# Edge scores of a graph layer's second stage moved from SBUF to a PSUM bank, and output stores that reuse a loaded register

## The chip, the cores and the metric

The kernel runs on one core of one Trainium2 chip. The metric is the device time of one execution in microseconds (us). Engines carry the profile's names: PE (matmuls), PEld (weight loads), DVE (VectorE), ACT (ScalarE), POOL (GpSimd) and SP (SyncE, which here only issues DMAs).

## What is computed

Two graph layers follow each other, each with a residual sum and a layer norm. There are 12500 nodes with 64 features and 200000 edges, sorted by destination. The change lies in the second layer, whose reference is, cut to what matters:

```python
Z = jnp.einsum('ni,rio->nro', h, fc_weight)        # 8 relations
z_s, z_d = Z[src, etype], Z[dst, etype]
aw = attn_weight[etype, :, 0]
e = relu(sum(concatenate([z_s, z_d], axis=1) * aw, axis=1))   # the score of an edge
m = segment_max(e, dst)
ex = exp(e - m[dst])
alpha = ex / segment_sum(ex, dst)[dst]
h_out = segment_sum(alpha[:, None] * z_s, dst)
x = layernorm(x + h_out)
```

So each edge has a score `e`, the maximum of the scores over the edges of one destination is subtracted, and the exponentials weigh the source rows.

## The kernel before

Edges are cut into chunks of 128 (one edge a partition). Four chunks are a run, two runs are a group, so a group is 8 chunks or 1024 edges, and there are 196 groups (`NG`). The destinations of a run lie in a window of `W` = 96 neighbouring nodes, so a sum or a maximum over destinations becomes work with 0/1 matrices of 128 edges by 96 nodes.

The first layer's loop (`sum0` and `finish0`, lines 480 to 506) writes a row of 65 numbers for each node and relation into `z_tab` in DRAM. The second layer's loop (lines 687 to 724) then runs over the 196 groups with `sum1`, and over 106 output tiles of 125 nodes with `finish1` and `scale1`. All are generators: each `yield` ends a piece, and the calls of `group(...)` and `node(...)` in lines 695 to 718 are the order of all instructions, written out by hand (`tc.manual_schedule()`), so that pieces of up to six groups stand between each other. Each engine works through its own instructions in that order.

What a group does, in `sum1`:

- POOL gathers the source rows: eight indirect DMAs a group, one for each chunk (line 311), into `zg`, which has 5 buffers; the index lists `row_i` lie in SBUF. Group i+3 is gathered while group i is worked on. SP loads the window's rows `dw` (line 530) and the row of relative destinations (line 444).
- PE and ACT build the transposed 0/1 matrix `ohT` (lines 539 to 543), DVE builds the 0/1 matrix `oh`, 128 x 768 (`choose`, line 305), out of a ramp of numbers `iota_n` that lies in the PSUM tile `psc`[...].
- DVE makes the scores `e`, 128 x 8 in SBUF: L560 sums the destination's part, L562 adds the source's part out of `zg` and is the first instruction of a group that waits for the gathers, and L563 takes the maximum with 0.
- DVE multiplies `oh` with the scores in two products of 128 x 384 (line 571): the first into the SBUF tile `oe`, the second into columns 128 to 511 of `psc`. L573 to L575 take the maximum over the four chunks of a run.
- The maximum over edges follows through a PE transpose (L580) and L585, and through L595 and L596 it meets the maxima `top` that were kept so far. L596 (`d`, 65 x 96, two for each group) subtracts one SBUF tile from another.
- L616 reads each edge's maximum out of PSUM into `em`, L617 subtracts it from `e`, ACT takes the exponential (L620) and scales `zg` with it (L622), PE sums over edges (L626), and L630 and L631 update the sums `acc` (SBUF) with numbers out of PSUM.

`finish1` loads a tile's rows `xn` at a node number that SP loads into a register out of `slot_row` (`slot`, line 431), and later computes the unscaled output `y`. For four tiles at once `scale1` takes the root and stores them: for each store SP loads the same node number out of `slot_row` again (line 670).

Of the kernel before, what the change touches and what calls it, by code (L numbers as in the profile page):

```python
# [29 lines left out]
AF = mybir.ActivationFunctionType  # L30
OP = mybir.AluOpType
AX = mybir.AxisListType
ENG = mybir.EngineType
PSUM = bass.MemoryType.PSUM

N, E, D, DE, NR = 12500, 200000, 64, 32, 8
P = 125
EC = 128
NT = N // P
KS = 4  # L40
RE = KS * EC
S = 2
K = S * KS
# [6 lines left out]
W = 96  # L50
# [10 lines left out]
def gnn_kernel(ctx: ExitStack, tc, x, xT, src, dstp, dst, et, eaT, u, W1, b1, W2, b2, fc, aw, out):  # L61
    nc = tc.nc
# [21 lines left out]
    iota = consts.tile([128, 128], F32, name="iota")  # L84
# [19 lines left out]
    nc.vector.memset(ones_row, 1.0)  # L104
    psc = fixed.tile([128, 512], F32, name="psc")

    nc.vector.tensor_copy(psc[:, :128], iota)
    iota_n, iota_r = psc[:EC, :W], psc[:EC, :NR]

    w1x = consts.tile([D, 2, D], F32, name="w1x")  # L110
# [45 lines left out]
    for j in range(4):  # L156
        s = slice(j * (N // 4), (j + 1) * (N // 4))
# [10 lines left out]
    with (  # L168
# [54 lines left out]
        at = pre.tile([NQ, RQ], F32, name="at")  # L223
# [54 lines left out]
    def window_of(row, at, *engines):  # L278
        return nc.values_load(row[0:1, at], engines=engines, min_val=0, max_val=N - 1,
                              skip_runtime_bounds_check_because="a destination, so a node")  # L280
# [149 lines left out]
    def slot(i):  # L430
        return lambda engine: nc.values_load(
            slot_row[0:1, i - FIRST:i - FIRST + 1], engines=[engine], min_val=0, max_val=N - P,
            skip_runtime_bounds_check_because="the first node of a tile")

    def span(g):

        n = min(S, NRE - g * S)
        return n, min(n * KS, NCE - g * K), slice(g * K, g * K + n * KS)

    def row_load(work, g):  # L440
        def load():
            n = span(g)[0]
            row = work.tile([1, n, RE], BF16, name="row", bufs=4)
            nc.sync.dma_start(row, rel_tab[g * S:g * S + n, :].rearrange("(o s) e -> o s e", o=1))
            return row
        return load

    def wins_load(g):
        return lambda engine: [window_of(base_row, slice(g * S + s, g * S + s + 1), engine) for s in range(span(g)[0])]

    def all_of(pieces):
        for _ in pieces:
            pass
# [10 lines left out]
    groups, slots = {}, {}  # L464
# [9 lines left out]
    with (  # L474
# [4 lines left out]
        psum = Banks(pool, {"po": "small", "pw": "small"})  # L479
        for i in range(-3, NG + 2):  # L480
            g = i + 3
            if g < NG:
                n, chunks, c = span(g)
# [39 lines left out]
    for t in (acc, top):  # L523
        nc.scalar.copy(t, none[:D + 1].to_broadcast([C, N + W]))

    def sum1(work, psum, n, chunks, idx, rel_of, et_of, row_of, wins_of):
        row = row_of()
        dw = work.tile([W, n, Q], BF16, name="dw", bufs=4)
        for s, b in enumerate(wins_of(ENG.SP)):
# [15 lines left out]
        pq = psum.tile([EC, n * KS, Q], F32, name="pq")  # L545
        for k in range(n * KS):
            s, i = divmod(k, KS)
            nc.tensor.matmul(pq[:, k, :], ohT[:, s, i * EC:(i + 1) * EC], dw[:, s, :], start=True, stop=True)
        yield
        oh = choose(work, rel_of, n, bufs=3)  # L550
# [8 lines left out]
        e = work.tile([EC, n * KS], F32, name="e")  # L559
        nc.vector.tensor_reduce(e, ed.rearrange("p k j r -> p k (j r)"), AX.X, OP.add)  # L560
        yield
        nc.vector.tensor_add(e, e, zg[:, :, D])  # L562
        nc.vector.scalar_tensor_tensor(e, e, 0.0, pq[:, :, 3 * NR], OP.max, OP.mult)  # L563


        half = KS // 2
        by_run, es = oh.rearrange("p (s i) w -> p s i w", s=n), e.rearrange("p (s i) -> p s i", s=n)
        oe = work.tile([EC, n, half, W], F32, name="oe")
        other = psc[:EC, 128:128 + n * half * W].rearrange("p (s i w) -> p s i w", s=n, i=half)
        for to, i in ((oe, slice(0, half)), (other, slice(half, KS))):  # L570
# [39 lines left out]
        for k in range(n * KS):  # L610
            s, i = divmod(k, KS)
# [2 lines left out]

        em = work.tile([EC, n * KS], F32, name="em")
        nc.vector.tensor_reduce(em, pm, AX.X, OP.add)  # L616
        nc.vector.tensor_sub(e, e, em)  # L617
        nc.scalar.activation(factor, d, AF.Exp)  # L618
        wz = work.tile([EC, n * KS, C], F32, name="wz")
        nc.scalar.activation(wz[:, :, D], e, AF.Exp)  # L620
        for k in range(n * KS):
            nc.scalar.activation(wz[:, k, :D], zg[:, k, :D], AF.Copy, scale=wz[:, k, D:])  # L622
        yield
        for k in range(n * KS):
            s, i = divmod(k, KS)
# [5 lines left out]
            nc.vector.tensor_add(mine, mine, sums[:, s, :])  # L631


    def finish1(work, psum, n0_of, y_of):

        n0 = n0_of(ENG.SP)
        xn = work.tile([P, D], F32, name="xn1", bufs=5)
        nc.sync.dma_start(xn, x1_tab[ds(n0, P), :])
        yield
        n0 = n0_of(ENG.Activation)  # L640
        own = work.tile([C, P], F32, name="own")
        nc.scalar.copy(own, acc[:, ds(n0, P)])
        yield
        pl = psum.tile([P, C], F32, name="pl")
        nc.tensor.transpose(pl, own, ident[:C, :C])
        yield
        y, mv = y_of()
        den = work.tile([P, 1], F32, name="den")

        nc.vector.tensor_scalar_max(den, pl[:, D:], 1e-30)  # L650
        nc.vector.reciprocal(den, den)
        nc.vector.scalar_tensor_tensor(y, pl[:, :D], den, xn, OP.mult, OP.add)
        st = work.tile([P, nc.vector.BN_STATS_DIM], F32, name="ln_st")
        nc.vector.bn_stats(out=st, in_=y)
        nc.vector.bn_aggr(out=mv, in_=st)

    def scale1(work, n0s_of, y, mv):
        n = len(n0s_of)
        v = work.tile([P, n], F32, name="ln_v")
        nc.scalar.activation(v, mv[:, :n, 1], AF.Sqrt, bias=eps)  # L660
        back = work.tile([1, 1], F32, name="back")
        nc.scalar.activation(back, none[:1], AF.Exp)  # L662
        yield
        nc.vector.reciprocal(v, v)
        shift = work.tile([P, n], F32, name="ln_shift")
        nc.vector.scalar_tensor_tensor(shift, mv[:, :n, 0], -1.0, v, OP.mult, OP.mult)
        yield
        for j, n0_of in enumerate(n0s_of):
            nc.scalar.activation(y[:, j, :], y[:, j, :], AF.Identity, bias=shift[:, j:j + 1], scale=v[:, j:j + 1])  # L669
            nc.sync.dma_start(out[ds(n0_of(ENG.SP), P), :], y[:, j, :])  # L670

    with (
        tc.tile_pool(name="l1", bufs=2) as work,
        tc.tile_pool(name="l1_ps", bufs=1, space=PSUM) as pool,
        tc.manual_schedule(),
    ):
        psum = Banks(pool, pq=2, pb=2)
        groups, slots, ys, scales = {}, {}, {}, {}

        def y_of(i):  # L680
            q, at = divmod(i - FIRST, NQ1)
            if at == 0:
                ys[q] = (work.tile([P, NQ1, D], F32, name="y1"),
                         work.tile([P, NQ1, nc.vector.BN_AGGR_DIM], F32, name="ln_mv"))
            return ys[q][0][:, at, :], ys[q][1][:, at, :]

        for i in range(-3, NG + 4):
            g = i + 3
            if g < NG:
                n, chunks, c = span(g)  # L690
                groups[g] = sum1(work, psum, n, chunks, row_i[:, c], rel[:, c], et_i[:, c],
                                 row_load(work, g), wins_load(g))
            if FIRST <= i < NG:
                slots[i] = finish1(work, psum, slot(i), lambda i=i: y_of(i))
            group(i + 3)
            node(i)
            group(i)
            group(i - 1)
            group(i + 2)
            group(i + 1)  # L700
            group(i + 2)
            node(i - 3)
            group(i)
            group(i + 2)
            group(i - 1)
            group(i - 1)
            group(i + 1)
            group(i)
            group(i)
            group(i - 1)  # L710
            group(i - 2)
            group(i - 1)
            group(i)
            node(i - 3)
            for q in scales:
                next(scales[q], None)
            group(i)
            node(i - 2)
            for q in scales:
                next(scales[q], None)  # L720
            q, at = divmod(i - 3 - FIRST, NQ1)
            if FIRST <= i - 3 < NG and (at == NQ1 - 1 or i - 3 == NG - 1):
                scales = {q: scale1(work, [slot(j) for j in range(i - 3 - at, i - 2)], *ys[q])}
                next(scales[q])

    with (
        tc.tile_pool(name="r1", bufs=1) as work,
        tc.tile_pool(name="r1_ps", bufs=1, space=PSUM) as psum,
    ):
        def more1(r, w):  # L730
            idx, rl, row, base = further(work, r, w)
            chunks = ds(r * KS, KS)
            etx = work.tile([EC, KS], I32, name="x_et")
            nc.vector.tensor_copy(etx, et_i[:, chunks])
            nc.vector.tensor_copy(idx, row_i[:, chunks])
            all_of(sum1(work, psum, 1, KS, idx, rl, etx, lambda: row, lambda engine: [base]))

        def node1(at):
            y = work.tile([P, 1, D], F32, name="y1")
            mv = work.tile([P, 1, nc.vector.BN_AGGR_DIM], F32, name="ln_mv")  # L740
            all_of(finish1(work, psum, lambda engine: at, lambda: (y[:, 0, :], mv[:, 0, :])))
            all_of(scale1(work, [lambda engine: at], y, mv))

        leftover(more1, node1)

# [41 lines left out]
```

## Time and profile before

| | |
|---|---|
| median of 3 runs | 4121.7 us (4120.01 to 4121.73) |
| the profiled execution | 4110.41 us, its span 4108.6 us |
| second layer's gathers on POOL | first starts at 2088.1 us, last at 4070.6 us; 1563, busy 1507.6 us |
| 2300 to 3100 us: busy of 800 us | PE 510, DVE 573, ACT 426, POOL 608 us |
| 3100 to 4000 us: busy of 900 us | PE 608, DVE 720, ACT 590, POOL 684 us |
| L571, first and second product | 558 and 560 ns, 195 full groups |
| L596 | 255 ns, 391 times |

In a group line of the profile the two numbers behind the first bar are the summed busy time in us and the mean of one instruction in ns; behind the second bar stands the idle time of the engine just before these instructions and what ended most of it. "issue" means that the engine waited for nothing that the profile shows. In a timeline the first number is the start in us from the span's start, the second the duration in us, and the bracket tells the idle time before. The profiled execution is 11.3 us shorter than the median of the timed runs.

### The profile page before, as it was taken

To read this page: it belongs to the slowest core of one execution; us is meant where nothing else is said; L and a number is where in the kernel's file an instruction comes from. 1 tells how busy PE (TensorE), PEld (TensorE's weight loads), DVE (VectorE), ACT (ScalarE), POOL (GpSimd) and SP (SyncE) were. 2 spreads that over 40 slices of the span, in tenths; PEclk is the share of its full clock that TensorE was granted. 3 is DMA by queue.
4 is the path that set the end of the run, shared out by engine and by line. 5 is a ranking of instruction groups with operands and counts; after the bars stand their busy time and mean duration, and the time that the engine had idled before them with its cause. 6 is when DMAs were issued, how large, how long until landed. Compare 5 with 4: busy or idle time off the path is not lost. (4 is left out here: it accounts for less than half of the span.)

```text
span 4108.6 us, 63192 instructions
## 1 busy us (share of the span) xinstructions
PE 2993.0 (73%) x16301; PEld 2321.8 (57%) x16302; DVE 2440.2 (59%) x8117; ACT 1432.1 (35%) x3693; POOL 2995.2 (73%) x3141
## 2 busy tenths in 40 slices
PE   4666776667899999999946666666567766666675
PEld 4555565556676777777735444444455544554454
DVE  3333333333555555555547777777778778878786
ACT  0000000000111111111155555555556666666665
POOL 1677777777777777777757777777777777777774
PEclk9655555555656555565555556555655556555655
DMA  5211111111333333333311111111111111111111
GB/s 132 53 45 45 46 45 45 45 46 46 73 78 78 77 78 78 81 80 78 75 37 29 29 29 28 28 29 28 29 31 35 35 35 35 35 34 36 34 36 26
DMA packets 316692, 201.40 MB, mean 49 GB/s; under 512 B 239185, under 2 KB 239315, under 8 KB 315966
## 3 DMA queue, kind: packets, MB, share of 16 engines
q0 software_dynamic: 100032, 103.43, 13.0%
q1 hardware_dynamic: 201039, 87.74, 8.6%
q10 hardware_dynamic: 15249, 6.10, 0.6%
q8 instruction: 132, 2.16, 0.2%
q14 instruction: 240, 1.97, 0.2%
HBM read 155.15 MB, written 41.84 MB: 48 GB/s over the span
## 5 line engine op out<-in xcount | busy, mean ns | idle before, releaser
L311 POOL DMA_INDIRECT bg<-b_tab,src_i x1563 | 1475.2, 944 | 574.6 <-issue 435.2
L311 POOL DMA_INDIRECT zg<-z_tab,row_i x1563 | 1507.6, 965 | 501.4 <-issue 423.1
L363 PE MATMUL pa<-oh,msg 128*64 128x96 f32 x3128 | 536.7, 364 | 276.0 <-ACT msg L358 273.2
L358 ACT ACTIVATE msg<-msg 128x512 f32<-128x512 f32 x196 | 123.2, 628 | 1709.1 <-DVE msg L357 1676.2
L353 PEld LDWEIGHTS pm<-aw,cb 128*128 128x128 f32 x3128 | 604.9, 297 | 138.6 <-issue 137.8
L363 PEld LDWEIGHTS pa<-oh,msg 128*64 128x64 f32 x3128 | 480.1, 222 | 297.6 <-ACT msg L358 291.1
L353 PE MATMUL pm<-aw,cb 128*128 128x64 f32 x3128 | 639.0, 389 | 0.0
L626 PE MATMUL pb<-oh,wz 128*65 128x96 f32 x3128 | 549.7, 369 | 16.1 <-ACT wz L622 3.0
L357 DVE TENSOR_TENSOR msg<-pm,bg 128x512 f32<-128x512 f32 x196 | 135.3, 690 | 698.9 <-DMA bg<-b_tab,src_i 553.7
L626 PEld LDWEIGHTS pb<-oh,wz 128*65 128x65 f32 x3128 | 494.6, 229 | 72.8 <-ACT wz L622 72.8
L622 ACT ACTIVATE wz<-zg,wz 128x64 f32<-128x64 f32 x1564 | 394.7, 335 | 6.7
L305 DVE TENSOR_TENSOR oh<-psc,rel 128x768 f32<-128x768 f32 x392 | 370.6, 945 | 12.3 <-DMA row<-rel_tab 9.5
L580 PE MATMUL pt<-ident,t 128*96 128x128 f32 x391 | 123.5, 419 | 326.6 <-DVE mq L375 326.3
L540 ACT ACTIVATE off<-ps_row,minus_p 96x512 bf16<-96x512 f32 x391 | 265.8, 680 | 264.1 <-PE ps_row L539 264.0
L539 PE MATMUL ps_row<-row,ones_row 1*96 1x512 bf16 x391 | 210.4, 538 | 196.5 <-ACT off L540 186.0
L369 DVE TENSOR_TENSOR xa<-xa,pa 64x96 f32 x391 | 100.8, 258 | 327.0 <-PE pa L363 319.5
L587 PE MATMUL pt<-ident,m 96*65 96x96 f32 x782 | 176.6, 380 | 159.6 <-DVE m L585 159.6
L580 PEld LDWEIGHTS pt<-ident,t 128*96 128x96 f32 x391 | 50.8, 184 | 418.6 <-issue 395.1
L348 DVE TENSOR_SCALAR cb<-ps_row,iota_p 96x1024 f32<-96x1024 f32 x196 | 246.1, 1256 | 9.0 <-PE ps_row L299 9.0
L587 PEld LDWEIGHTS pt<-ident,m 96*65 96x65 f32 x782 | 119.6, 220 | 176.8 <-DVE m L585 176.8
L299 PE MATMUL ps_row<-row,ones_row 1*96 1x512 bf16 x391 | 197.8, 604 | 17.5 <-DMA row<-rel_tab 16.2
L543 ACT ACTIVATE ohT<-off 96x1024 bf16<-96x1024 bf16 x196 | 206.6, 1054 | 6.3
(140 smaller groups left out, 3613.5 us busy)
## 6 DMA issues: line engine op xcount, KB each, us to landing
z_tab<-z SPq DMA_DIRECT2D x106, 253.9 KB
bg<-b_tab,src_i POOLq DMA_INDIRECT x1563
zg<-z_tab,row_i POOLq DMA_INDIRECT x1563
cb<-in_eaT SPq DMA_DIRECT2D x195, 128.0 KB
aw<-a_tab SPq DMA_DIRECT2D x391, 24.0 KB
dw<-d_tab SPq DMA_DIRECT2D x391, 4.7 KB
row<-rel_tab SPq DMA_DIRECT2D x390, 2.0 KB
xn<-in_x SPq DMA_DIRECT2D x106, 31.2 KB
```

The costliest lines, as they stand in the source:

```text
L299: nc.tensor.matmul(ps[:, s, :RE], ones_row, row[:, s, :], start=True, stop=True)
L305: nc.vector.tensor_tensor(oh, iota_n[:, None, :].to_broadcast([EC, n * KS, W]), rel_of.unsqueeze(2).to_broadcast([EC, n * KS, W]), OP.is_e ...
L311: nc.gpsimd.indirect_dma_start(out=to[:, k, :], out_offset=None, in_=table[:, :], in_offset=bass.IndirectOffsetOnAxis(ap=idx[:, k:k + 1], ...
L348: nc.vector.tensor_scalar(cb[:W, :, :], ps_row, iota_p[:W], None, OP.is_equal)
L353: nc.tensor.matmul(pm[:, k, :], cb[:, s, i * EC:(i + 1) * EC], aw_t[:, s, :], start=True, stop=True)
L363: nc.tensor.matmul(pa[D:, s, :], msg[:, k, :], oh[:, k, :], start=(i == 0), stop=(i == KS - 1))
L539: nc.tensor.matmul(ps_row[:, :RE], ones_row, row[:, s, :], start=True, stop=True)
L540: nc.scalar.activation(off[:, s, :], ps_row[:, :RE], AF.Abs, bias=minus_p[:W])
L543: nc.scalar.activation(ohT, off, AF.Relu, bias=1.0, scale=-1.0)
L587: nc.tensor.matmul(rows[:, s, :], m[:, s:s + 1].to_broadcast([W, C]), ident[:W, :W], start=True, stop=True)
L622: nc.scalar.activation(wz[:, k, :D], zg[:, k, :D], AF.Copy, scale=wz[:, k, D:])
L626: nc.tensor.matmul(sums[:, s, :], wz[:, k, :], oh[:, k, :], start=(i == 0), stop=(i == KS - 1))
```

## The change

The scores of a group leave L563 into columns 96 to 103 (even group) or 104 to 111 (odd group) of the PSUM tile `psc`, no longer into the SBUF tile `e`. Both products and the later subtraction (L617) read them there. The subtraction's result goes into `em`, and ACT's exponential reads `em`. The ramp copied into `psc` is cut from 128 to 96 columns to make room. Apart from that, `finish1` hands on the register with the node number, and `scale1` stores with it, so that the second register load for each store is gone.

```diff
-    nc.vector.tensor_copy(psc[:, :128], iota)
+    nc.vector.tensor_copy(psc[:, :W], iota[:, :W])
...
-    def sum1(work, psum, n, chunks, idx, rel_of, et_of, row_of, wins_of):
+    def sum1(work, psum, n, chunks, idx, rel_of, et_of, row_of, wins_of, odd=0):
...
         nc.vector.tensor_add(e, e, zg[:, :, D])
-        nc.vector.scalar_tensor_tensor(e, e, 0.0, pq[:, :, 3 * NR], OP.max, OP.mult)
+        score = psc[:EC, W + odd * K:W + odd * K + n * KS]
+        nc.vector.scalar_tensor_tensor(score, e, 0.0, pq[:, :, 3 * NR], OP.max, OP.mult)
...
-        by_run, es = oh.rearrange("p (s i) w -> p s i w", s=n), e.rearrange("p (s i) -> p s i", s=n)
+        by_run, es = oh.rearrange("p (s i) w -> p s i w", s=n), score.rearrange("p (s i) -> p s i", s=n)
         oe = work.tile([EC, n, half, W], F32, name="oe")
         other = psc[:EC, 128:128 + n * half * W].rearrange("p (s i w) -> p s i w", s=n, i=half)
         for to, i in ((oe, slice(0, half)), (other, slice(half, KS))):
             nc.vector.tensor_mul(to, by_run[:, :, i, :], es[:, :, i].unsqueeze(3).to_broadcast([EC, n, half, W]))
...
-        nc.vector.tensor_sub(e, e, em)
+        nc.vector.tensor_sub(em, score, em)
...
-        nc.scalar.activation(wz[:, :, D], e, AF.Exp)
+        nc.scalar.activation(wz[:, :, D], em, AF.Exp)
...
-    def finish1(work, psum, n0_of, y_of):
+    def finish1(work, psum, n0_of, y_of, tell=lambda n0: None):
...
         nc.sync.dma_start(xn, x1_tab[ds(n0, P), :])
+        tell(n0)
...
-        for j, n0_of in enumerate(n0s_of):
+        for j, n0 in enumerate(n0s):
...
-            nc.sync.dma_start(out[ds(n0_of(ENG.SP), P), :], y[:, j, :])
+            nc.sync.dma_start(out[ds(n0, P), :], y[:, j, :])
...
-                slots[i] = finish1(work, psum, slot(i), lambda i=i: y_of(i))
+                slots[i] = finish1(work, psum, slot(i), lambda i=i: y_of(i), lambda n0, i=i: places.update({i: n0}))
...
-                scales = {q: scale1(work, [slot(j) for j in range(i - 3 - at, i - 2)], *ys[q])}
+                scales = {q: scale1(work, [places[j] for j in range(i - 3 - at, i - 2)], *ys[q])}
```

More of the change, by code (lines that the diff above doesn't have):

```diff
@@ L655, in finish1, with scale1 @@
         nc.vector.bn_aggr(out=mv, in_=st)
-    def scale1(work, n0s_of, y, mv):
-        n = len(n0s_of)
+    def scale1(work, n0s, y, mv):
+        n = len(n0s)
         v = work.tile([P, n], F32, name="ln_v")
@@ L677, in gnn_kernel @@
         psum = Banks(pool, pq=2, pb=2)
-        groups, slots, ys, scales = {}, {}, {}, {}
+        groups, slots, ys, scales, places = {}, {}, {}, {}, {}
         def y_of(i):
@@ L691, in gnn_kernel @@
                 groups[g] = sum1(work, psum, n, chunks, row_i[:, c], rel[:, c], et_i[:, c],
-                                 row_load(work, g), wins_load(g))
+                                 row_load(work, g), wins_load(g), g % 2)
             if FIRST <= i < NG:
-                slots[i] = finish1(work, psum, slot(i), lambda i=i: y_of(i))
+                slots[i] = finish1(work, psum, slot(i), lambda i=i: y_of(i), lambda n0, i=i: places.update({i: n0}))
             group(i + 3)
@@ L741, in node1 @@
             all_of(finish1(work, psum, lambda engine: at, lambda: (y[:, 0, :], mv[:, 0, :])))
-            all_of(scale1(work, [lambda engine: at], y, mv))
+            all_of(scale1(work, [at], y, mv))
         leftover(more1, node1)
```

## The prediction

> **What bounds the kernel now.** I read the page first: its groups, then the list of waits, then the timeline of single engines in the second layer, since the change touches nothing that runs often before it (the ramp's copy runs once, at 285 ns). On the page the dearest group after 2088 us is the gathers:
>
> ```profile
> span 4108.6 us, 63192 instructions
> ...
> L311 POOL DMA_INDIRECT zg<-z_tab,row_i x1563 | 1507.6, 965 | 501.4 <-issue 423.1
> ```
>
> 1507.6 us busy and 501.4 us idle fill the stretch from 2088.1 us to 4071.8 us, in which the last gather ends (25.3 us of the idle time is the stage's begin). So POOL does nothing else there, and its idle time is said to wait for nothing. The list of waits confirms who waits for whom:
>
> ```profile
> POOL zg L311 <- issue: 423.1, 1306, 25.3
> ...
> DVE e L562 <- DMA zg<-z_tab,row_i: 245.0, 182, 2.2
> ```
>
> In 182 of 196 groups DVE stands at L562 until the gathers have landed, 1.39 us in the median. The next view is POOL's timeline of one group and a bit:
>
> ```profile
> 3000.34 0.94 POOL L311 DMA_INDIRECT zg<-z_tab,row_i  x1 [0.30 <-issue]
> 3001.59 0.94 POOL L311 DMA_INDIRECT zg<-z_tab,row_i  x1 [0.30 <-issue]
> 3002.83 0.94 POOL L311 DMA_INDIRECT zg<-z_tab,row_i  x1 [0.30 <-issue]
> 3004.08 1.11 POOL L311 DMA_INDIRECT zg<-z_tab,row_i  x1 [0.30 <-DMA zg<-z_tab,row_i]
> 3005.50 0.94 POOL L311 DMA_INDIRECT zg<-z_tab,row_i  x1 [0.31 <-issue]
> 3006.74 0.94 POOL L311 DMA_INDIRECT zg<-z_tab,row_i  x1 [0.30 <-issue]
> 3007.99 0.94 POOL L311 DMA_INDIRECT zg<-z_tab,row_i  x1 [0.30 <-issue]
> 3009.24 0.94 POOL L311 DMA_INDIRECT zg<-z_tab,row_i  x1 [0.30 <-issue]
> 3010.49 0.95 POOL L311 DMA_INDIRECT zg<-z_tab,row_i  x1 [0.30 <-issue]
> ```
>
> The reader is to see two things. The gap is 0.30 us whatever the bracket says: over all 1563 gathers it never exceeds 0.32 us after the first, so no buffer and no DMA holds POOL (a `zg` buffer has been free for 10.7 us or more when its gather starts). And one gather in eight, the third of a group, takes 1.11 us instead of 0.94. Its mean over 196 groups is 1103 ns; the other positions have a median of 944 ns. The excess over 944 ns of all 1563 gathers is 1507.6 - 1563 x 0.944 = 32.1 us, of which 196 x 0.159 = 31.2 us is the third one's. What ran on DVE in that stretch:
>
> ```profile
> 3002.95 0.17 DVE L562 TENSOR_TENSOR e<-e,zg 128x8 f32<-128x8 f32 x1 [1.40 <-DMA zg<-z_tab,row_i]
> 3003.15 0.16 DVE L563 SCALAR_TENSOR_TENSOR e<-e,pq 128x8 f32<-128x8 f32 x1
> 3003.35 0.56 DVE L571 TENSOR_TENSOR oe<-oh,e 128x384 f32<-128x384 f32 x1
> 3003.83 0.56 DVE L571 TENSOR_TENSOR psc<-oh,e 128x384 f32<-128x384 f32 x1
> ...
> 3006.13 0.95 DVE L305 TENSOR_TENSOR oh<-psc,rel 128x768 f32<-128x768 f32 x1
> ...
> 3007.96 0.25 DVE L631 TENSOR_TENSOR acc<-acc,pb 65x96 f32 x1
> ...
> 3009.00 0.25 DVE L596 TENSOR_TENSOR d<-top,most 65x96 f32<-65x96 f32 x1
> ```
>
> The second product, with both inputs (`oh` and `e`) in SBUF, began at 3003.83 and was still running when the gather began at 3004.08. L305 likewise covers the start of the gather at 3006.74, and L631 that at 3007.99, and neither stretches it: one input of each lies in PSUM. I sorted all gathers of the trace by the DVE instruction that was running at their start and ended over 150 ns later:
>
> ```
> running on DVE          inputs            gathers  ran on, mean  stretch over 942 ns, mean
> L571 psc<-oh,e          SBUF, SBUF            170        316 ns                   177.5 ns
> L571 oe<-oh,e           SBUF, SBUF             11        308 ns                   183.0 ns
> L596 d<-top,most        SBUF, SBUF             18        225 ns                    48.5 ns
> L631 acc<-acc,pb        SBUF, PSUM            160        213 ns                     1.5 ns
> L305 oh<-psc,rel        PSUM, SBUF (both layers)  177    about 710 ns               1.6 ns
> L573 psc<-oe,psc        SBUF, PSUM              6        296 ns                     2.0 ns
> ```
>
> The single cases give the law: the gather is late by the time that the instruction runs on after the gather's start, less 134 ns (L571) or 122 ns (L596). If that instruction began less than 40 ns before the gather, the gather isn't stretched and the instruction takes some 30 ns more.
>
> **What the Trainium skill says.** "SBUF — State Buffer", section "Who interferes with whom": a DVE instruction with two SBUF inputs contends with a GpSimd instruction that reads SBUF, and with at most one SBUF input it doesn't (outside the 2-port modes). The trace agrees, 177.5 against 1.5 ns. The same section infers that descriptor generation isn't held by a tensor_tensor; the trace differs for these gathers, which read an index list. "VectorE: DVE Perf Modes", section "The perf-mode tier table": an f32 tensor_tensor runs at one element a cycle with SBUF and with PSUM operands. The trace agrees: L574 and L575, with one PSUM input, take 353 ns for 192 elements, and L571 558 ns for 384, 1.07 ns for each further element. The same page, section "The DRAIN you can't avoid": a semaphore between DVE instructions costs nothing extra. Here the trace differs: where the next instruction has no wait it starts 81 ns before the recorded end of the last (L571 to L571), with one 35 ns after it.
>
> **The change, part by part.**
> - *Products read scores from PSUM.* The two-SBUF products were 196 pairs; now each has one PSUM input and should be as harmless as L631. Ceiling: the 32.1 us. Their own duration, 558 and 560 ns: between L574 (353 ns for 192 elements) and L305 (947 for 768), both with one PSUM input, 384 elements come to 551 ns, 560 with a PSUM output (next point), so between -7 and 0 ns; I take 0.
> - *L563 writes PSUM.* L573 against L574 shows 9 ns more for a PSUM output with the same inputs. 196 x 9 ns lies in DVE's slack at L562: nothing. L617 has one SBUF input less; same duration, 170 ns, and its six covers stretched nothing (2.0 ns).
> - *An added wait.* In the changed program's instruction list the second product of a group now waits on DVE's own semaphore; before it waited for nothing. Both products now read the bank that it writes. It costs 81 + 35 = 116 ns for each group, 22.7 us of DVE in all. Queued behind it is DVE's whole rest of the group (L573 up to the next L562) and, through `t`, `m` and `em`, PE's L580 and ACT's L618 to L622. The cover is the 1.39 us at L562: less 0.16 us for the shorter period and 0.116 us, some 1.1 us stay (0.6 us in the groups with a table load, which had 0.85 to 0.9). A late group is caught by the 10.7 us that POOL has on its buffers. No other wait is added on PE, DVE, ACT or POOL. Without cover it would cost the 22.7 us.
> - *What falls on a gather's start next.* Gathers four to eight of a group now start about 0.16 us sooner against DVE, and DVE's work after the products lies 0.116 us later. L596 is the remaining two-SBUF instruction of length. I replayed each group: gathers at 1.249 us spacing, DVE times from the trace, moved by 116 ns, stretch by the law above. With nothing moved the replay of before gives 32.06 us against the 32.1 measured. After, it gives 0.9 us: the first L596 now mostly begins after the seventh gather's start, at which it ended before. With a delay of 0 ns it would be 4.6 us (92 groups touched), with 40 ns 3.9, with 200 ns 0.4. I take 1.0; bounds 0.1 and 4.6.
> - *Stores.* 106 register loads of some 0.56 us leave SP (60 us of its queue). In the tail they lie within the 1.65 us from store to store, which is the landing of the store before: a load ends 0.92 us after its store's issue began, the landing wait about 1.6 us after. So they are hidden, 0; if that cover were gone, the last five would be worth 5 x 0.56 = 2.8 us. What they let start sooner behind them are `row`, `dw` and `xn` loads, which feed PE and DVE, not POOL: 0. No DMA is added or moved past another.
> - *Tail.* After the last gathers the chain that ended last passes two groups' L571 pairs: 2 x 0.116 = +0.2 us. The shorter ramp copy saves some 30 ns once.
>
> Sum: -32.1 + 1.0 + 0.2 = -30.9 us against the profiled execution, 4110.4 to 4079.5 (span 4077.7). The timed median lies 11.3 us above that execution; nothing in the sum depends on it, so the same difference is taken from it: 4121.7 - 30.9 = 4090.8.
>
> **Rivals.**
> - *A: the collision moves to L596 for most groups*, since the DVE delay isn't what I think (the replay is worst between 0 and 40 ns) or ACT shifts it. For: it stretched 12 gathers by 50 to 93 ns before. At 60 ns in every group: 196 x 0.06 = 11.8 us given back, 4102.6. Against: its spread over groups lets only some fall in the bad 0.2 us.
> - *B: the hold isn't a matter of where the scores lie* but of this product as such, broadcast operand and 384 columns. Then the added wait makes the second product end 116 ns later past the same gather's start, and with 174 groups stretched: 174 x 0.116 = +20.2 us, 4141.9. It decides as soon as a product with a PSUM input stretches a gather at all. Against: L305 has a broadcast PSUM input and 768 columns and stretches nothing, though no case in before has a broadcast second input from PSUM.
> - *C: no difference*, because gathers are paced by something that the records show as busy time, and a freed 0.16 us is waited out elsewhere: 4121.7. Against: the seven other gathers keep 1.249 us without fail.
> - *D, part of B's side: DVE becomes the bound.* It needs over 1.1 us more in a group, that is products of twice their length; L573 to L575 speak against it. I give it no chance of its own.
>
> **How the numbers follow.** My case 0.80, A 0.12, B with D 0.05, C 0.03. The smallest difference that can be told from none for this kernel is about 0.2%, 8.2 us: faster is below 4113.5, so my case and A, 0.92; same 0.03; slower 0.05. The range: my case runs from 4089.9 (all 32.1 gone) to 4094.6 (residue 4.6) and some 5 us either way for runs and placement (three runs of before differ by 1.7 us); up to A's 4103 above, 4085 below. That leaves out B, C and little else.
>
> **What would show it.** In the profile after: third gathers at 944 ns, the group mean near 945 ns and 1477 us busy; L571 unchanged in length but 35 ns after its predecessor; L562 waiting about 1.1 us for the gathers; a few seventh gathers stretched; SP's second loads gone with the stores' spacing still 1.65 us. It is wrong if the third gather stays above 1 us (B), if the sixth to eighth grow (A), or if POOL's gaps grow past 0.32 us (C, D).

## The result and the profile after

| | before | after |
|---|---|---|
| median of 4 runs each | 4121.72 us (4120.01 to 4121.76) | 4077.54 us (4076.02 to 4082.93) |
| ratio after to before | | 0.9896, 95% interval 0.9879 to 0.9913 |
| the profiled execution: its time, its span | 4110.41, 4108.6 us | 4077.9, 4076.2 us |
| first gather of the second layer | 2088.1 us | 2088.6 us |
| from there to the end of the last gather | 1983.7 us | 1951.0 us |
| from there to the end | 36.9 us | 36.5 us |

The kernel became faster by 44.2 us. The forecast was 30.9 us, 4090.8 us with a range from 4085.0 to 4103.0, so the side was right and the size was not: the time lies 7.5 us below the range. The two profiled executions differ by 32.4 us only, nearly what was forecast for them. So the missing 13.3 us are not in these two profiles; most of them are the 11.3 us by which the timed runs of before were longer than its profiled execution. The changed kernel has no such gap: its profiled execution takes what its other runs take.

Where the 32.4 us went, page and list of waits of the changed kernel show (L312 is the gather, L563 the first instruction that waits for it; lines have moved by one or two):

```profile
span 4076.2 us, 63086 instructions
...
L312 POOL DMA_INDIRECT zg<-z_tab,row_i x1563 | 1475.0, 944 | 501.3 <-issue 418.1
```

```profile
DVE e L563 <- DMA zg<-z_tab,row_i: 178.7, 171, 2.1
```

The mean gather is 944 ns, POOL's busy time is 32.6 us shorter, its idle time is the same to 0.1 us. DVE still waits for the gathers in 171 groups, 178.7 us in all in place of 245.0. In the order of instructions POOL is three groups ahead of the group that DVE works on, as the kernel's description has it. In time it is not: L562 of a group starts 2.62 us after that same group's last gather, so the third gather, which the second product stretched, is that of the next group. The timeline of POOL and DVE in the changed kernel has the collision still in it, without its cost (L573 are the products, L598 the former L596):

```profile
3006.24 0.95 POOL L312 DMA_INDIRECT zg<-z_tab,row_i  x1 [0.30 <-issue]
...
3008.74 0.94 POOL L312 DMA_INDIRECT zg<-z_tab,row_i  x1 [0.30 <-issue]
...
3009.99 0.94 POOL L312 DMA_INDIRECT zg<-z_tab,row_i  x1 [0.30 <-DMA zg<-z_tab,row_i]
3011.23 0.94 POOL L312 DMA_INDIRECT zg<-z_tab,row_i  x1 [0.30 <-issue]
```

```profile
3008.93 0.17 DVE L563 TENSOR_TENSOR e<-e,zg 128x8 f32<-128x8 f32 x1 [1.06 <-DMA zg<-z_tab,row_i]
3009.13 0.17 DVE L565 SCALAR_TENSOR_TENSOR psc<-e,pq 128x8 f32<-128x8 f32 x1
3009.34 0.55 DVE L573 TENSOR_TENSOR oe<-oh,psc 128x384 f32<-128x384 f32 x1
3009.93 0.56 DVE L573 TENSOR_TENSOR psc<-oh,psc 128x384 f32<-128x384 f32 x1
```

The second product began at 3009.93 and ran until 3010.49, across the start of the gather at 3009.99, and the gather took 0.94 us. In the whole trace 137 gathers began under a second product that ran on for 479 ns in the mean; their stretch is 1.1 ns.

One number in this view was not in the forecast. L563 starts 0.19 us after the gather before it (3008.93 against 3008.74); in the profile of before L562 started 0.12 us after it. Over all groups, from the start of a group's last gather to the first instruction that waits for it: 2.62 us in the profile of before, 2.70 us in that of after. The gathers landed some 80 ns later. In a kernel whose collisions depend on when DVE is released, that is a suspect for the 11 us.

### The profile page after: what moved, and what is told of

Read it like the earlier page. It is cut to its first block, busy times and chain, and to the rows that moved or that the text cites. A ratio compares the mean times of both kernels' runs of the same rounds, so it can differ in the third digit from the quotient of the medians.

```text
span 4076.2 us, 63086 instructions
## 1 busy us (share of the span) xinstructions
PE 3003.9 (74%) x16301; PEld 2327.4 (57%) x16302; DVE 2465.0 (60%) x8117; ACT 1432.2 (35%) x3693; POOL 2962.8 (73%) x3141
## 5 line engine op out<-in xcount | busy, mean ns | idle before, releaser
L312 POOL DMA_INDIRECT bg<-b_tab,src_i x1563 | 1475.4, 944 | 575.0 <-issue 448.3
L312 POOL DMA_INDIRECT zg<-z_tab,row_i x1563 | 1475.0, 944 | 501.3 <-issue 418.1
```

The lines of the kernel that those rows point to most:

```text
L312: nc.gpsimd.indirect_dma_start(out=to[:, k, :], out_offset=None, in_=table[:, :], in_offset=bass.IndirectOffsetOnAxis(ap=idx[:, k:k + 1], ...
```

## The experiments

**The theory** is the phase. In before, what a third gather loses is the time by which the second product outlasts the gather's start, and that product is released by the landing of the gathers. Where they land later, it outlasts more, up to the point at which it begins after the gather's start. I replayed the trace of before as in the prediction, with all DVE work of a group later by L: the stretch is 32.1 us at L = 0, 37.2 at 40 ns, 40.9 at 65 ns and 43.5 at 84 ns. **The first rival**: the 11 us lie elsewhere, in the first layer, in the tail or in the stores, and the stretch is 32 us in the timed runs too. **The second rival**: two SBUF inputs cost POOL by their running time, not by their place, so each product has a share.

**Before once more, on stalling chips.** The kernel before and the change's parts ran together on one chip. What was expected of before, and of the parts:

> The kernel before, unchanged, profiled again. Theory (phase): the timed runs of before are 11.3 us longer than its profiled execution because there the gathers land later, so DVE's second product starts later and runs on further past the third gather's start. The first L562 to last gather's start was 2.62 us in the profile of before and 2.70 us in the profile of after. Replaying before's trace with all DVE work of a group 84 ns later gives 43.5 us of stretch in place of 32.1. So: about 4121 us, third gathers at some 1160 ns in the mean in place of 1103, second layer's gathers over 1995 us in place of 1983.7, first layer and tail as before. Rival (elsewhere): third gathers at 1103 ns again, and the 11 us in the first layer (gathers begin at 2099 us in place of 2088) or in the tail after the last gather (48 us in place of 36.9).

> Only the stores' part of the change: the second register load of each store is gone, the scores stay in SBUF. Theory: hidden behind the landing of the store before, so the same time as before within 3 us, about 4121 us, spacing of stores 1.65 us still. Rival (the missing 13 us come from the stores, which free SP's queue by 60 us): about 4108 us.

> Only the scores' part of the change, stores as in before. Theory: all of the gain, 4075 to 4083 us, no gather stretched. Rival (the stores share in it): about 4091 us.

> The change, but the first product reads its scores in SBUF again (L563 is done twice, once into PSUM, once into SBUF, some 0.2 us more of DVE in each group), the second in PSUM. Theory (only what is running at a gather's start and has two SBUF inputs counts; that was the second product in 170 groups of 196): 4 to 5 us of stretch by the replay, since the first product, 0.2 us later, now ends just past some third gathers' starts; 4077 + 5 = about 4082 us. Rival (each product with two SBUF inputs costs by itself): half of the gain, about 4099 us.

Their edits: the first has none. The second has the lines of the diff with `tell`, `places` and `n0s`; the third has all the others. The fourth is the third plus stores, with the first product as before:

```diff
         nc.vector.scalar_tensor_tensor(score, e, 0.0, pq[:, :, 3 * NR], OP.max, OP.mult)
+        nc.vector.scalar_tensor_tensor(e, e, 0.0, pq[:, :, 3 * NR], OP.max, OP.mult)
...
+        eb = e.rearrange("p (s i) -> p s i", s=n)
...
-        for to, i in ((oe, slice(0, half)), (other, slice(half, KS))):
-            nc.vector.tensor_mul(to, by_run[:, :, i, :], es[:, :, i]...)
+        for to, i, by in ((oe, slice(0, half), eb), (other, slice(half, KS), es)):
+            nc.vector.tensor_mul(to, by_run[:, :, i, :], by[:, :, i]...)
```

None of the four told what it was meant to tell, for on that chip before took 5421.56 us. The page of before there and a stretch of its timeline:

```profile
span 5416.2 us, 63192 instructions
...
L311 POOL DMA_INDIRECT zg<-z_tab,row_i x1563 | 1506.7, 964 | 1316.8 <-ACT top L597 798.1
```

```profile
4005.69 0.16 DVE L375 CAST mq<-pb 96x2 bf16<-96x2 f32 x1 [7.25 <-remote]
4005.73 0.68 ACT L540 ACTIVATE off<-ps_row,minus_p 96x512 bf16<-96x512 f32 x1 [10.02 <-remote]
```

The mean gather is as long as in the first profile, but POOL is idle for 1316.8 us in place of 501.4. In the stretch shown DVE stood still for 7.25 us and ACT for 10.02, and PE, which is not shown, for 10.53, all at the same time; "remote" means that the profile can't name what ended the wait. POOL then waits for ACT, whose L622 is the last to read a `zg` buffer. Stretches of over 1 us without any work on PE, DVE and ACT come to 1161 us after the first 60 us; in the first profile to 191 us, all of it in the first layer. POOL is not the bound there. The three parts ran again, with the same edits:

> The stores' part alone once more, since in the first attempt all kernels were held up by stalls on that chip. Theory: no gain, 4120 us within 3; spacing of stores in the tail 1.65 us as before, third gathers stretched as in before. Rival (the stores share in the missing 13 us): about 4108 us.

> The scores' part alone once more. Theory: all of the gain, 4077 us within 3, no gather stretched. Rival (the stores share in it): about 4088 us.

> The second product alone from PSUM once more (the first reads the scores in SBUF, L563 is done twice). Theory: 4 to 5 us of stretch, left by the first product, 4082 us within 3. Rival (each product with two SBUF inputs costs by itself): half of the gain, about 4099 us.

This was one more chip with stalls. A third time:

> The stores' part alone, a third time, for a chip without stalls. Theory: no gain, 4120 us within 3; gathers stretched by 40 us as in before, stores in the tail 1.65 us apart. Rival (the stores share in the missing 13 us): about 4108 us.

> The scores' part alone, a third time. Theory: all of the gain, 4077 us within 3, no gather stretched. Rival (the stores share in it): about 4088 us.

> The second product alone from PSUM, a third time. Theory: 4 to 5 us of stretch, left by the first product, 4082 us within 3. Rival (each product with two SBUF inputs costs by itself): half of the gain, about 4099 us.

The third chip stalled too. The nine runs of parts on these chips:

| | stores alone | scores alone | second product alone |
|---|---|---|---|
| first chip, before 5421.56 us | 0.9993 (0.9981 to 1.0006) | 0.9813 (0.9793 to 0.9833) | 0.9878 (0.9860 to 0.9897) |
| second, before 5438.19 us | 0.9997 (0.9986 to 1.0009) | 0.9852 (0.9829 to 0.9875) | 0.9895 (0.9878 to 0.9911) |
| third, before 5424.55 us | 0.9996 (0.9984 to 1.0008) | 0.9794 (0.9767 to 0.9820) | 0.9855 (0.9821 to 0.9890) |

(Before against itself on the first: 1.0004, 0.9992 to 1.0016.) The stores bring nothing on any of them. The scores bring 78 to 117 us there, more than the whole stretch of the gathers; why, and what stops the engines, these runs don't show, and the account of the collision below does not rest on them.

**Before, delays, and the changed kernel on one chip.** Four kernels on a chip without the stalls, on which before took 4121.24 us (18 runs), as in the result.

> The kernel before, unchanged, profiled once more. Theory (phase): what a gather loses to the second product depends on how late the gathers of a group land. L = how much later L562 starts after the last gather's start than the 2.62 us of the first profile. By the replay the gathers' stretch is 32.1 us at L = 0, 37.2 at 40 ns, 40.9 at 65 ns, 43.5 at 84 ns, and the time above that of a kernel without stretch follows it: with this run's own L the stretch is on that curve within 2 us. Rival (elsewhere): the stretch is 32 us whatever L, and what differs between runs lies in the first layer or the tail.

No edit. Measured 4119.84 us, ratio 0.9997 (0.9987 to 1.0006). Its page has

```profile
span 4118.5 us, 63192 instructions
...
L311 POOL DMA_INDIRECT zg<-z_tab,row_i x1563 | 1517.0, 971 | 501.3 <-issue 422.7
```

and its timeline one collision, to be read beside that of the first profile:

```profile
3007.79 0.94 POOL L311 DMA_INDIRECT zg<-z_tab,row_i  x1 [0.30 <-issue]
3007.92 0.17 DVE L562 TENSOR_TENSOR e<-e,zg 128x8 f32<-128x8 f32 x1 [1.43 <-DMA zg<-z_tab,row_i]
...
3008.80 0.56 DVE L571 TENSOR_TENSOR psc<-oh,e 128x384 f32<-128x384 f32 x1
...
3009.03 1.14 POOL L311 DMA_INDIRECT zg<-z_tab,row_i  x1 [0.30 <-issue]
```

The same program, the same first layer (gathers of the second begin at 2088.4 us), the same tail (37.0 us), the same idle time of POOL, but 1517.0 us of gathers in place of 1507.6. L, the time by which the gathers land later, is 71 ns here (2.693 against 2.622 us in the median), the replay gives 42.0 us of stretch at 71 ns, and 1517.0 - 1563 x 0.944 is 41.5 us. The mean third gather takes 1153 ns, 209 ns more than the others; in the first profile it was 159 ns more. The rival that put the difference elsewhere falls for these two profiles: 9.4 of the 9.9 us between the two spans are gather time.

It is the transfer that is slower, not DVE's answer to it. The queue that carries the gathers of both layers moved the same packets in both profiles (the last number is the time that they took, as a share of the span of 16 DMA engines; the first profile, then this one):

```profile
q0 software_dynamic: 100032, 103.43, 13.0%
...
q0 software_dynamic: 100032, 103.43, 15.9%
```

Between 2100 and 4000 us a packet of it took 88.6 ns in the mean in the first profile and 111.2 ns in this one. The last packet of a group ended 2.07 and 2.14 us after its last gather's start, and L562 followed 0.55 us later in both. What makes the packets slower is not shown.

> Before, with L563 done twice in each group (the second time changes no number): the products and all DVE work after them start 0.197 us later, nothing else changes, and DVE has 39 us more to do. Theory (phase): the second product now mostly begins after the third gather's start, or less than 40 ns before, and then holds nothing. Replay: stretch 41 us at L = 0, 24 at 40 ns, 13 at 65 ns, 11 at 84 ns, against 32 to 43 of before; at L = 65 to 84 ns it is 28 to 32 us FASTER than before, at L = 0 it is 9 us slower. Rival (two SBUF inputs cost POOL by their mere running time): the same as before within 3 us. Rival (DVE's work counts): slower by up to 39 us.

```diff
         nc.vector.scalar_tensor_tensor(e, e, 0.0, pq[:, :, 3 * NR], OP.max, OP.mult)
+        nc.vector.scalar_tensor_tensor(e, e, 0.0, pq[:, :, 3 * NR], OP.max, OP.mult)
```

Measured 4091.99 us, ratio 0.9941 (0.9922 to 0.9961): 196 more instructions on DVE, and 29 us less. Gathers and collision (L572 are the products here):

```profile
span 4090.2 us, 63388 instructions
...
L311 POOL DMA_INDIRECT zg<-z_tab,row_i x1563 | 1489.5, 953 | 499.9 <-issue 418.0
```

```profile
3006.27 0.94 POOL L311 DMA_INDIRECT zg<-z_tab,row_i  x1 [0.30 <-issue]
3006.30 0.57 DVE L572 TENSOR_TENSOR psc<-oh,e 128x384 f32<-128x384 f32 x1
```

The product with two SBUF inputs now begins 30 ns after the gather and holds nothing, in this group. In other groups it begins ahead of the gather, and this trace shows where the hold sets in: second products that began up to 30 ns before the gather left it at its usual 0.94 us, though they ran on past its start, and took 597 to 626 ns themselves in place of 559; the 15 that began 31 to 50 ns before it made it 1.32 to 1.34 us long. Stretch 1489.5 - 1475.5 = 14.0 us; the replay has 12.6 us for 71 ns. Both rivals that count DVE's work or the products' running time fall with this run.

> Before, with L563 done three times: products 0.394 us later, 77 us more of DVE. Theory (phase): the second product is out of the way, the first product now runs over the third gather's start. Replay: stretch 19 us at L = 0, 25 at 40 ns, 29 at 65 ns, 32 at 84 ns: faster than before by 11 to 13 us, and slower than with one delay if L is 65 ns or more. The rivals as in the run with one delay.

The same line three times in all. Measured 4108.11 us, ratio 0.9970 (0.9959 to 0.9981), 13 us less than before and 16 us more than with one delay, as expected. The first product has moved over the third gather's start: 154 gathers began under it, with a stretch of 171.5 ns in the mean against 171 by the law (it ran on 305 ns, less 134). Stretch in all 1504.1 - 1475.5 = 28.6 us, replay 30.1.

> The changed kernel on the same chip as these three. Theory: no gather stretched whatever L, 1951 us for the gathers of the second layer, and shorter than before on this chip by the whole stretch that the before of this call shows plus 0 to 1 us of tail. Rival (elsewhere): shorter by 32 us only, or by more than the stretch of before.

Measured 4077.97 us, ratio to before 0.9902 (0.9882 to 0.9921). Its profile's span is 44.0 us below that of the first run of this group. Gathers of the second layer: 1950.9 us against 1993.1, which is 42.2 of the 44.0; the rest is 1.3 us in the first layer and 0.4 us in the tail. The gathers land as late as in that run (2.70 us), and their stretch is 0.2 us in all.

**The parts on a chip with early landings.** On another chip without stalls before took 4109.71 us in the median of 13 runs, not 4121. Twelve of them took 4107.4 to 4111.2 us, and one 4118.94.

> The stores' part alone, a fourth time. Theory: no gain, 4120 us within 3; gathers stretched by 40 us as in before, stores in the tail 1.65 us apart. Rival (the stores share in the missing 13 us): about 4108 us.

Measured 4108.96 us, ratio 0.9999 (0.9989 to 1.0008): no share. That it is also the number of the rival is chance, since before itself takes 4109.71 us on this chip. Its trace, which is before's but for the stores, has L = 3 ns (2.625 us), and gathers as in the first profile:

```profile
span 4106.8 us, 63086 instructions
...
L311 POOL DMA_INDIRECT zg<-z_tab,row_i x1563 | 1507.5, 964 | 500.3 <-issue 421.3
```

Stores in its tail stand 1.65 us apart as before, the wait for the landing longer by what the load took. The 4120 us that were expected were those of a chip with late landings.

> The scores' part alone, a fourth time, for a chip without stalls. Theory: all of the gain, 4077 us within 3, no gather stretched. Rival (the stores share in it): about 4088 us.

Measured 4079.58 us, ratio 0.9927 (0.9908 to 0.9947): 30.1 us less than before on this chip. POOL's gathers take 1477.4 us in its profile, 30.1 us less than those of the stores alone:

```profile
span 4078.8 us, 63192 instructions
...
L312 POOL DMA_INDIRECT zg<-z_tab,row_i x1563 | 1477.4, 945 | 499.6 <-issue 417.3
```

So a kernel without these collisions ends at nearly the same time on both chips (4079.58 us here, 4077.97 for the whole change on the chip with late landings), and the gain is what before had lost on that chip.

> The second product alone from PSUM, a fourth time. Theory: 4 to 5 us of stretch, left by the first product, 4082 us within 3. Rival (each product with two SBUF inputs costs by itself): half of the gain, about 4099 us.

Measured 4085.27 us, ratio 0.9940 (0.9921 to 0.9960): 24.4 of the 30.1 us, not half of them; it is 0.3 us above the range that was expected. Stretch 1479.9 - 1475.5 = 4.4 us, replay 3.9 at L = 0. In 24 groups the first product, 0.2 us later by the doubled L563, lies over a gather's start, with 213 ns of stretch in the mean. The rest of the difference to the scores alone is within the spread of three runs.

## Why the prediction was right in kind and wrong in size

- *What bounds the kernel, and what the change frees.* Right. POOL's gathers pace the second layer, there only instructions with two SBUF inputs stretch them by more than 17 ns, and a PSUM operand ends that: the mean stretch under a second product went from 177.5 to 1.1 ns. (In the first layer a copy with one SBUF input, L389, stretched 8 gathers by 12 ns in the mean; the change doesn't touch it.) Rival B, a product that holds gathers wherever its scores lie, is refuted by the same number.
- *The ceiling, "the 32.1 us".* Right for the execution that it was read from, and on the chip with early landings, where the gain of the scores was 30.1 us against 30.9. It is the mis-sized term for the timed runs: on the chip with late landings it measured 41.5 us.
- *The step that failed* is "nothing in the sum depends on it, so the same difference is taken from it", said of the 11.3 us between the profiled execution and the median. The sum did depend on it. The law that the prediction itself had read from single cases says that a gather loses what the product outlasts; so 70 to 80 ns of later landing, in some 170 groups, are 12 to 14 us, less what is saved where the product no longer begins ahead of the gather. The replay, run for L = 0 alone, had the answer in it: 43.5 us at 84 ns, about what the profile of after shows. Shown is that one program has both: 32.1 us of stretch with early landings, 41.5 us with late ones, and next to none in the changed kernel with either. That the timed runs of before had late landings is inferred, since they were not traced: they took 4120.0 to 4121.8 us, as the kernel did on the chip with late landings (4121.24 in the median). The remaining 2 us or so of the 44.2 lie in the first layer, the tail and the spread of the runs; no run separates them.
- *The law.* Its slope holds (171.5 ns measured against 171 with two delays), and the limit of 40 ns fits L596 (41 ns let through, 45 held) and the first product (42 let through, 51 held), but for the second product it is 31. An instruction that begins within the limit takes some 40 to 75 ns more, not some 30. Both are small here. The table's row for L305 is short: by its own rule the trace has 347 gathers and not 177, 190 of them in the second layer, with the same 1.5 ns of stretch.
- *The range* had 5 us either way "for runs and placement". That was a guess where a number stood on the page: the 11.3 us, in a kernel whose other runs agree within 1.8 us. (Its 4094.6 for a residue of 4.6 us is 4094.4 by its own terms; nothing turns on that.)
- *The added wait.* Right: the second product starts 36 ns after the first's end (3009.34 + 0.55 to 3009.93), and DVE's wait at L563 fell to 1.04 us in the median (1.1 expected). It costs POOL no time.
- *L596 and rival A.* Right to the microsecond or so: 1.0 us was taken, and the gathers of after show less than 0.2 us of stretch.
- *Durations from PSUM.* L573 took 553 and 562 ns in the median (551 and 560 expected), L565 171 ns in place of 163, L619 167 ns.
- *Stores.* Right: 0.9999 on the one chip, 0.9993 to 0.9997 on the three others.

## What to carry to other kernels

If POOL's gathers pace a stage, look for the one gather of the period that is longer than the rest, and for the DVE instruction with two SBUF inputs that began before it; one operand moved to PSUM ends it. The instruction itself took as long as before; here a wait came with it, 116 ns of DVE for each group, which DVE's wait for the gathers covered. A loss that depends on the phase of two engines is not a constant: replay it over the shifts that runs can have before the number is used. Where the profiled execution and the timed runs differ by more than the runs do among themselves, find the term that differs, or take the difference into the range.

## What was not expected of the hardware

- The same gathers landed some 70 to 80 ns later in some profiles than in others (2.62 and 2.625 us from start to the first user, against 2.69 to 2.70). With the same program that goes with 4110 and 4121 us. All four profiles of one chip were late and all three of another early; but one run of 13 on the second took 4118.94 us, so it isn't shown that the chip alone decides.
- A gather isn't held by an instruction with two SBUF inputs that begins less than 31 to some 45 ns before it (31 for the second product, some 45 for L596), nor by one that begins after it: with L572 30 ns behind the gather's start, both took their usual time to 0.01 us. So doing L563 twice made the kernel before 29 us faster, with late landings. With early ones the replay has it 9 us slower, which was not run.
- Three chips stopped PE, ACT and DVE together for 5 us in the mean in the first layer and 2.5 to 4.9 us in the second, about a thousand us in all, released by nothing that the profile names. What it is stays open.
